# Attention's head norm in a macaron block: squares and last product on GpSimd, inverse roots spread over partitions by DMA

## The chip, the core and the metric

The kernel runs on one core of a Trainium2 chip. Five engines work side by side, each through its own instructions in the program's order: TensorE (PE; its weight loads are shown as PEld), VectorE (DVE), ScalarE (ACT), GpSimd (POOL) and SyncE (SP), which here only issues DMAs. They wait for each other through semaphores. The metric is the device time of one execution in microseconds (us); less is better.

## The reference, cut to what matters

The input x is 8 batches of 512 tokens of 512 values, in float32. Three parts follow each other, each added to x: half of a mixture-of-experts layer, differential attention, and half of the mixture-of-experts layer again. What the change touches is the norm of each head's output in attention:

```python
q, k = _rope(q), _rope(k)
energy = einsum('bqhad,bkhad->bahqk', qd, kd)             # two maps per head
scores = softmax(where(causal, NEG, energy) / sqrt(D))
diff = softmax(where(causal, NEG, scores[:, 0] - lam * scores[:, 1]))
att = einsum('bhqv,bvhd->bqhd', diff, v)                  # 16 heads of D = 32
att = att * rsqrt(mean(att * att, axis=-1) + EPS) * rms_w # the head norm
return (att * (1 - LAM_INIT)).reshape(b, s, E) @ Wo
```

## The kernel before

**Stages.** The first mixture-of-experts layer runs ahead of attention, the second partly beside its end and partly behind it. x stays in SBUF all the time. Attention works through its 8 batches one after the other; each has two phases (head groups gp = 0 and 1) and each phase 11 blocks, 176 blocks in all. A token tile is 128 tokens, so a batch has four tiles (i = 0 to 3); a block holds some heads' queries of one tile against the keys that these may see.

**The loop over blocks** stands in `attention` at L1068 to L1124, and the order of every engine's work is the order in which it is written there (a manual schedule). In round k different blocks are at different steps: scores of block k + 1 (PE, L761), energies of block k (DVE, L777: score plus causal mask, and the smallest value of a row), first exponentials of block k (ACT, L790), mask (POOL, L828), factors (DVE L799, POOL L804) and weighing (POOL, L814) of block k - 1, difference of block k - 1 (DVE, L848), second exponentials of block k - 2 (ACT, L862), transposes of block k - 3 (PE, L882; copies on DVE L898 and ACT L900), and the product with the values of block k - 4 (PE, L913), copied on DVE into the tile "aT" (L926).

**Slots.** All other work of attention is put into named slots of a round: `at(o, slot, fn)` puts fn into round o of a phase, and `fill(k, slot)` runs what is there. In the order of a round the slots are "short" (early on PE), "act mid", "mid", "long", "long 2" (PE), "dve", "act" and "pool". The slot "pool" comes last in a round, behind the difference, and its instructions are made to wait for that difference (`after=u1["diff"]`). So on POOL they stand between the weighing of one block and the mask of the next.

In these slots are: the layer norm of the next batch ("h", L574 on POOL), the projections with rope (`rope_steps`: product "r_ps" L635 on PE, two products with cosine and sine on DVE L654 and L656, two DMAs on SP that swap neighbouring partitions, "r_sw" from "r_by" L662, and an addition on POOL L665), the value projection (L610), and `finish_steps`, which the change is about. PSUM has eight banks; four hold scores, two the transposes, and the two of `misc` go in turn to every product of the slots and to the products with the values.

**The head norm, `finish_steps` (L672 to L747),** runs once per batch and tile, 32 times. "aT" has the heads' values along partitions: partition 32 q + d, four chunks c along the free side, so 16 heads, and 128 tokens.

- square (slot "act", round o0): ACT squares aT into "f_sq" (L683, 128x512) and two small squares of the softmax sums z2 into "f_u" (L685), which carry EPS.
- sums (slot "short", round o1): PE sums the squares over each head's 32 partitions with "hsum" (L694) and adds the EPS part (L700), into "f_ss"; head (c, q) comes out on partition 32 c + q.
- root (slot "act mid", round o1): ACT makes the inverse root as exp(-0.5 ln) into "f_r" (L707, L708).
- turn (slot "short", round o3): PE spreads each head's row over its 32 partitions again, 16 products with one column of the identity that is read with step zero 32 times, into "f_f" in PSUM (L715).
- norm (slot "dve", round o3): DVE multiplies aT by f_f into "f_an" (L723).
- pe (slots "long" and "long 2", round o4): PE multiplies by Wo into "f_o" (L731), and DVE adds the result to x one round later (L737).

The rounds are given where it is called:

```python
finish_steps(at, (0, 1, 2, 4, 5) if b < B else LAST[0], b - 1, 2, sts[b - 1])
finish_steps(at, (3, 5, 5, 7, 8) if b < B else LAST[1], b - 1, 3, sts[b - 1])
...
finish_steps(at, (4, 5, 5, 7, 9), b, 0, sts[b])
finish_steps(at, (6, 7, 7, 9, 10), b, 1, sts[b])
```

Tiles 0 and 1 are finished in the second phase of their batch, tiles 2 and 3 in the first phase of the next; the last batch's tiles 2 and 3 in the drain behind all blocks.

Of the kernel before, what the change touches and what calls it, by code (L numbers as in the profile page):

```python
# [9 lines left out]
F32 = mybir.dt.float32  # L10
# [6 lines left out]
P = 128  # L17
# [24 lines left out]
def macaron_kernel(  # L42
# [61 lines left out]
    nc.vector.tensor_scalar(root_eps, parity, RMS_EPS**0.5, None, ALU.mult)  # L104
    both = keep.tile([P, Q], F32, name="both")
    nc.vector.tensor_tensor(both, of_head[:, 0], of_head[:, 1], ALU.add)
    ln_eps = keep.tile([P, 1], F32, name="ln_eps")
    nc.gpsimd.memset(ln_eps, LN_EPS)

# [43 lines left out]
        "S6 T72 L70 X T73 P1 L73 X S7 P2",  # L153
    )

    LAST = ((0, 1, 1, 2, 3), (3, 4, 4, 5, 6))

    KEPT = 6
    ctx.enter_context(tc.manual_schedule())
# [383 lines left out]
    def attention(f0, f1, home, first_end, projections_end, drain):  # L543
# [128 lines left out]
        def finish_steps(at, os, b, i, st):  # L672

            name = f"f{b}_{i}"
            t = {}

            def square():
                t["sq"] = home["sq"].tile([P, 4, P], F32, name=f"{name}_sq", tag="sq", bufs=2)

                t["u"] = tiny.tile([P, 2, 4, 4], F32, name=f"{name}_u", tag="u")  # L680
                z2 = st["z2"][:, i * H : (i + 1) * H]
                uh = t["u"].rearrange("p f c (q h) -> p (f c q) h", h=2)
                nc.scalar.activation(t["sq"], st["aT"][i], AF.Square)  # L683
                for h in range(2):
                    nc.scalar.activation(  # L685
                        uh[:, :, h], z2, AF.Square, scale=root_eps[:, h : h + 1]
                    )

            def sums():


                t["ss"] = misc(f"{name}_ss")
                for c in range(4):
                    nc.tensor.matmul(  # L694
                        t["ss"][32 * c : 32 * (c + 1), :P], hsum, t["sq"][:, c, :],
                        start=True, stop=False, tile_position=(0, 32 * c),
                    )
                for f in range(2):
                    for c in range(4):
                        nc.tensor.matmul(  # L700
                            t["ss"][32 * c : 32 * c + 4, f * Q : (f + 1) * Q], t["u"][:, f, c],
                            both, start=False, stop=(f == 1), tile_position=(0, 32 * c),
                        )

            def root():
                r = t["r"] = tiny.tile([P, P], F32, name=f"{name}_r", tag="r")
                nc.scalar.activation(r, t["ss"][:, :P], AF.Ln, bias=idle)  # L707
                nc.scalar.activation(r, r, AF.Exp, scale=-0.5)  # L708

            def turn():  # L710

                t["f"] = misc(f"{name}_f")
                for c in range(4):
                    for q in range(4):
                        nc.tensor.matmul(  # L715
                            t["f"][q * D : (q + 1) * D, c * P : (c + 1) * P],
                            ident[:, 32 * c + q : 32 * c + q + 1].to_broadcast([P, D]), t["r"],
                            start=True, stop=True, tile_position=(0, q * D),
                        )

            def norm():
                t["an"] = home["sq"].tile([P, 4, P], F32, name=f"{name}_an", tag="sq", bufs=2)
                nc.vector.tensor_tensor(  # L723
                    t["an"], st["aT"][i], t["f"].rearrange("p (c q) -> p c q", c=4), ALU.mult
                )

            def pe(h):
                if h == 0:
                    t["o"] = misc(f"{name}_o")
                for c in (2 * h, 2 * h + 1):  # L730
                    nc.tensor.matmul(  # L731
                        t["o"], t["an"][:, c, :], wo_sb[:, c // 2, c % 2, :],
                        start=(c == 0), stop=(c == 3),
                    )

            def residual():
                nc.vector.tensor_add(x_sb[b][:, i, :], x_sb[b][:, i, :], t["o"])  # L737

            o0, o1, o2, o3, o4 = os
            at(o0, "act", square)  # L740
            at(o1, "short", sums)
            at(o1, "act mid", root)
            at(o3, "short", turn)
            at(o3, "dve", norm)
            at(o4, "long", lambda: pe(0))
            at(o4, "long 2", lambda: pe(1))
            at(o4 + 1, "mid", residual)  # L747

# [136 lines left out]
        def turn_copy(u, par):  # L887
            nr, i, np = u["nr"], u["i"], u["pairs"]
            o = u["unit"]["eT"][:, par]
            s = u["tp"][par][:, : (i + 1) * nr * P]  # L890
            if nr > np:
                o = o[:, 0].rearrange("p r f t -> p f r t")
                s = s.rearrange("p (f r t) -> p f r t", f=2, r=np)
            else:
                o = o[:, :, :, u["parts"][0].half]
                s = s.rearrange("p (c r t) -> p c r t", c=i + 1, r=nr)
            if par == 0:
                nc.vector.tensor_copy(o, s)  # L898
            else:
                nc.scalar.copy(o, s)  # L900
# [85 lines left out]
        def plan(ph):  # L986

            b, gp = divmod(ph, 2)
            at = placer(starts[ph])
            if gp == 0:  # L990
                if b < B:
                    for n, o in enumerate((0, 0, 1, 2, 3)):
                        rope_steps(at, o, b, 1, n, sts[b])
                    if b + 1 < B:
                        sts[b + 1] = new_batch()
                        norm_steps(at, b + 1, sts[b + 1])
                if b > 0:
                    finish_steps(at, (0, 1, 2, 4, 5) if b < B else LAST[0], b - 1, 2, sts[b - 1])
                    finish_steps(at, (3, 5, 5, 7, 8) if b < B else LAST[1], b - 1, 3, sts[b - 1])
            else:  # L1000
                if b + 1 < B:
                    for n, o in enumerate((0, 1, 1, 2, 4)):
                        rope_steps(at, o, b + 1, 0, n, sts[b + 1])
                    value_steps(at, 3, b + 1, sts[b + 1])
                finish_steps(at, (4, 5, 5, 7, 9), b, 0, sts[b])
                finish_steps(at, (6, 7, 7, 9, 10), b, 1, sts[b])
                if b == B - 1:
                    for n, os in enumerate(EARLY):
                        early_steps(at, n, *os)
# [58 lines left out]
        for k in range(K + 13):  # L1068
# [38 lines left out]
                turn_copy(u2, 0)  # L1107
            if u2 is not None:
                turn_copy(u2, 1)
            fill(k, "long")  # L1110
            if place == 1:
                scores_next(k)
# [89 lines left out]
    def first_end():  # L1202
        first_y.close()
        opened["out"], opened["blocks"] = pool("out", "right"), pool("blocks", "right")
        home.update(aT=opened["out"], sq=opened["out"], h=(opened["out"], "sq"))
        home.update(dict.fromkeys(("kq1", "v", "e", "t", "eT"), opened["blocks"]))

    def projections_end():
# [134 lines left out]
```

## Time and profile before

| what | us |
|---|---|
| median of 3 runs | 1421.32 (1421.29 to 1422.11) |
| profiled execution, from first to last instruction | 1420.2 |
| first layer, start of the projections | 0 to about 210 |
| attention's blocks | about 210 to 1260 |
| rest of the second layer and output | about 1260 to 1420 |

Of the profiled execution only the span is recorded. The operations of the head norm in it:

| operation | engine | count | mean ns |
|---|---|---|---|
| f_sq (L683) | ACT | 32 | 632 |
| f_u (L685) | ACT | 64 | 302 |
| f_ss (L694, L700) | PE | 256, 512 | 283, 222 |
| f_r (L707, L708) | ACT | 32, 32 | 363, 311 |
| f_f (L715) | PE | 1024 | 278 |
| f_an (L723) | DVE | 32 | 683 |
| f_o (L731) | PE | 256 | 605 |

TensorE's instructions overlap, so their count times their mean is more than PE's busy time: f_f takes 35.0 us of PE in all. How to read the views: an engine's busy share is over the whole span; the windows give the same by stage; the chain of work that ended last says, step by step, which piece of work released the next one; in the timeline each line is start, length, engine, line, operation and tiles, and in brackets the idle time ahead of it with what ended it.

### The profile page before, as it was taken

The numbers are of one execution on the slowest core, as the hardware profiler recorded it, in microseconds if no ns is written. First come the engines' busy times: TensorE is split into PE (matmuls) and PEld (weight loads), VectorE is DVE, ScalarE is ACT, GpSimd is POOL, SyncE is SP. The second block draws the span as 40 slices with busy tenths as digits, with TensorE's granted clock in tenths as the row PEclk, the third lists the DMA queues.
The fourth block names the chain that finished last, engine by engine and source line by source line (L and its number), as shares of the span: only waits on it lengthen the run. The fifth ranks groups of instructions, "written<-read, shape, count | busy, mean of one in ns | idle before, by whom it ended". The sixth has DMA issues, their size and how long they took to land.

```text
span 1420.2 us, 30675 instructions
## 1 busy us (share of the span) xinstructions
PE 1328.5 (94%) x9774; PEld 738.4 (52%) x9774; DVE 1154.9 (81%) x4405; ACT 1047.0 (74%) x3644; POOL 685.4 (48%) x1314
## 2 busy tenths in 40 slices
PE   6999899899999999999999999999999997998998
PEld 4544444455555555555555555555455555555443
DVE  6554769899989988998999899889989989654566
ACT  3411128999899898989898998989899989844110
POOL 5433626554555455454545555554545555443230
PEclk9999988999999999999999999999999997999999
DMA  9300011000000101000000001010000001000006
GB/s 344 91 1 0 0 38 38 9 31 24 16 24 17 39 1 38 9 31 9 32 24 16 28 13 39 2 38 16 24 13 27 28 13 40 1 5 1 1 1 236
DMA packets 27554, 48.19 MB, mean 34 GB/s; under 512 B 4720, under 2 KB 6016, under 8 KB 27392
## 3 DMA queue, kind: packets, MB, share of 16 engines
q1 hardware_dynamic: 25152, 42.03, 8.3%
q10 hardware_dynamic: 2208, 4.19, 0.8%
q8 instruction: 77, 1.26, 0.4%
q14 instruction: 85, 0.70, 0.2%
q0 software_dynamic: 32, 0.01, 0.0%
HBM read 16.86 MB, written 8.39 MB: 18 GB/s over the span
## 4 chain that ended last, share of the span: by engine, by line
PE 60%; ACT 13%; DVE 10%; issue 2%; POOL 0%; ACTq 0%; DVEq 0%
PE r_ps L635 18%; PE sc L761 8%; PE f_o L731 8%; ACT e L790 7%; PE tp L882 6%; PE yps L381 6%; PE av L913 4%; DVE e L777 4%; DVE t L848 3%; ACT t L862 2%; PE vps L610 2%; PE kps L403 2%; PE f_f L715 1%; ACT eT L900 1%; PE tp L325 1%
## 5 line engine op out<-in xcount | busy, mean ns | idle before, releaser
L790 ACT ACTIVATE e<-e,nb 128x192 f32<-128x192 f32 (+7 forms) x1024 | 535.5, 532 | 6.5 <-DVE nb L777 4.3
L777 DVE CUSTOM_DVE_ANT_0 e<-sc,mpos 128x192 f32<-128x192 f32 (+7 forms) x1024 | 400.8, 453 | 23.7 <-PE sc L761 16.5
L814 POOL TENSOR_SCALAR e<-e,z 128x512 f32<-128x512 f32 (+7 forms) x512 | 295.9, 590 | 16.7
L862 ACT ACTIVATE t<-t,nm 128x512 f32<-128x512 f32 (+7 forms) x512 | 270.0, 534 | 42.2 <-DVE nm L848 42.0
L761 PE MATMUL sc<-r,r 32*128 32x64 f32 (+7 forms) x2048 | 245.3, 456 | 10.8 <-DVE nb L777 4.9
L848 DVE CUSTOM_DVE_ANT_0 t<-e,z 128x512 f32<-128x512 f32 (+7 forms) x512 | 240.6, 518 | 5.1 <-POOL e L814 4.2
L635 PE MATMUL r_ps<-hT,wq_sb 128*128 128x512 f32 x512 | 235.6, 601 | 0.1
L381 PE MATMUL yps<-we,y 128*128 128x512 f32 x456 | 216.5, 612 | 1.0 <-ACT y L388 0.7
L882 PEld LDWEIGHTS tp<-ident,t 128*128 128x128 f32 x1280 | 146.5, 144 | 135.6 <-ACT eT L900 43.3
L882 PE MATMUL tp<-ident,t 128*128 128x128 f32 x1280 | 188.6, 283 | 28.1 <-ACT eT L900 26.6
L790 ACT ACTIVATION_READ_ACCUMULATOR e<-e,nb 128x1 f32 x1024 | 202.1, 197 | 0.0
L665 POOL TENSOR_TENSOR r<-r,r_sw 128x512 f32<-128x512 f32 x80 | 103.0, 1296 | 175.8 <-DVE z L799 84.2
L761 PEld LDWEIGHTS sc<-r,r 32*128 32x128 f32 x2048 | 117.4, 188 | 90.7 <-DVE nb L777 44.6
L391 POOL TENSOR_TENSOR y<-y,eb 128x512 f32<-128x512 f32 x57 | 73.1, 1283 | 164.4 <-ACT y L388 134.3
L635 PEld LDWEIGHTS r_ps<-hT,wq_sb 128*128 128x128 f32 x512 | 93.0, 190 | 113.9 <-issue 99.6
L388 ACT COPY y<-yps 128x512 f32<-128x512 f32 x57 | 33.4, 586 | 155.6 <-PE yps L381 155.6
L828 POOL TENSOR_SCALAR_AFFINE_SELECT e<-e 128x128 f32<-128x128 f32 x256 | 79.2, 316 | 99.4 <-ACT e L790 99.4
L898 DVE COPY eT<-tp 128x512 f32<-128x512 f32 (+1 forms) x176 | 112.0, 636 | 16.6 <-PE tp L882 16.6
L381 PEld LDWEIGHTS yps<-we,y 128*128 128x128 f32 x456 | 81.3, 192 | 78.4 <-issue 73.6
L731 PE MATMUL f_o<-wo_sb,f_an 128*128 128x512 f32 x256 | 118.6, 605 | 0.0
L804 POOL TENSOR_TENSOR z<-z,over 128x4 f32<-128x4 f32 (+1 forms) x192 | 38.0, 201 | 142.6 <-DVE z L799 142.5
L862 ACT ACTIVATION_READ_ACCUMULATOR t<-t,nm 128x1 f32 x512 | 100.4, 196 | 0.0
(123 smaller groups left out, 1668.6 us busy)
## 6 DMA issues: line engine op xcount, KB each, us to landing
r_sw<-r_by SPq DMA_DIRECT2D x160, 128.0 KB, 2.0
x<-in_x_dram SPq DMA_DIRECT2D x6, 1024.0 KB, 13.2
out_dram<-x SPq DMA_DIRECT2D x6, 512.0 KB, 3.2
out_dram<-x ACTq DMA_DIRECT2D x6, 512.0 KB, 3.2
x<-in_x_dram SPq DMA_DIRECT2D x8, 256.0 KB, 8.2
we<-in_expert_w_dram SPq DMA_DIRECT2D x2, 1024.0 KB, 7.7
wq_sb<-in_wq_dram SPq DMA_DIRECT2D x1, 2048.0 KB, 13.9
wo_sb<-in_wo_dram SPq DMA_DIRECT2D x8, 128.0 KB, 2.8
```

The costliest lines, as they stand in the source:

```text
L381: nc.tensor.matmul(held["yps"], buf[b][:, i, c * P : (c + 1) * P], held["we"][:, c, :], start=(c == 0), stop=(c == EC - 1),)
L635: nc.tensor.matmul(t["ps"], w[:, c, c0 : c0 + P], st["hT"][:, c, :], start=(c == 0), stop=(c == EC - 1),)
L665: return nc.gpsimd.tensor_add(t["out"], t["out"], t["sw"])
L731: nc.tensor.matmul(t["o"], t["an"][:, c, :], wo_sb[:, c // 2, c % 2, :], start=(c == 0), stop=(c == 3),)
L761: nc.tensor.matmul(u["sc"][j][:, part.cols], q[j * D : (j + 1) * D, q0 : q0 + P], kq["k"][j * D : (j + 1) * D, : part.n], start=True, stop ...
L777: nc.vector.tensor_tensor_reduce(out=u["e"][:, j, part.cols], in0=u["sc"][j][:, part.cols], in1=mpos[:, S - part.n :], scale=1.0, scalar=3 ...
L790: nc.scalar.activation(e, e, AF.Exp, bias=u["nb"][:, c : c + 1], scale=-1.0, accum_out=u["z"][:, 0, c : c + 1],)
L814: nc.gpsimd.tensor_scalar(e, e, u["z"][:, 1, c : c + 1], u["z"][:, 0, c - nr : c - nr + 1], ALU.mult, ALU.mult,)
L848: u["diff"] = nc.vector.tensor_tensor_reduce(out=u["t"][:, par, r * w : r * w + part.n], in0=u["e"][:, 2 * par, s], in1=u["e"][:, 2 * par ...
L862: nc.scalar.activation(t, t, AF.Exp, bias=u["nm"][:, par, r : r + 1], scale=-1.0, accum_out=z2[:, col : col + 1],)
L882: nc.tensor.transpose(u["tp"][par][:, o : o + P], u["t"][:, par, (r * (i + 1) + c) * P : (r * (i + 1) + c + 1) * P], ident,)
L898: nc.vector.tensor_copy(o, s)
```

## The change

Thirty of the 32 head norms change; tiles 2 and 3 of the last batch keep the way of before, under the names `square_late`, `turn_late` and `norm_late`. In the others:

- square goes from ACT (slot "act") to POOL (slot "pool", same round): one 128x512 product of aT with itself, a 128x16 product of z2 with itself, and a 128x32 product of that with the new constant "eps_of".
- sums stays in its round or comes one earlier, but goes from the slot "short" to a new slot "sums", behind the transposes' copies and ahead of "long"; root goes from "act mid" to "act".
- turn and its 16 products on PE go. In their place SP issues four DMAs, one per chunk c: four rows of f_r are each written to 32 partitions of f_sq (64 KB). They follow the root in program order.
- norm goes from DVE (slot "dve") to POOL (slot "pool"), in place in f_sq, in the round after the root. That is two to one rounds earlier than before; pe stays where it was.
- The normalised input "h" gets its own buffers; before it shared those of "sq".

```diff
-    LAST = ((0, 1, 1, 2, 3), (3, 4, 4, 5, 6))
+    LAST = ((0, 1, 2, 3), (3, 4, 5, 6))
...
             def square():
                 t["sq"] = home["sq"].tile([P, 4, P], F32, name=f"{name}_sq", tag="sq", bufs=2)
+                first = nc.gpsimd.tensor_tensor(t["sq"], st["aT"][i], st["aT"][i], ALU.mult)
                 z2 = st["z2"][:, i * H : (i + 1) * H]
+                zz = tiny.tile([P, H], F32, name=f"{name}_zz", tag="zz")
+                nc.gpsimd.tensor_tensor(zz, z2, z2, ALU.mult)
+                nc.gpsimd.tensor_tensor(
+                    factor_tile(), zz.unsqueeze(2).to_broadcast([P, H, 2]),
+                    eps_of.unsqueeze(1).to_broadcast([P, H, 2]), ALU.mult,
+                )
+                return first
...
+            def spread():
+                for c in range(4):
+                    nc.sync.dma_start(
+                        t["sq"][:, c, :],
+                        t["r"][32 * c : 32 * c + 4, :].unsqueeze(1).to_broadcast([4, D, P]),
+                    )
+
+            def norm():
+                t["an"] = t["sq"]
+                return nc.gpsimd.tensor_tensor(t["an"], t["an"], st["aT"][i], ALU.mult)
+
-            def turn():
+            def turn_late():
...
-            o0, o1, o2, o3, o4 = os
-            at(o0, "act", square)
-            at(o1, "short", sums)
-            at(o1, "act mid", root)
-            at(o3, "short", turn)
-            at(o3, "dve", norm)
-            at(o4, "long", lambda: pe(0))
...
+            o0, o1, o2, o3 = os
+            if b == B - 1 and i > 1:
+                at(o0, "act", square_late)
...
+            else:
+                at(o0, "pool", square)
+                at(o1, "sums", sums)
+                at(o1, "act", root)
+                at(o1, "act", spread)
+                at(o2, "pool", norm)
+            at(o3, "long", lambda: pe(0))
...
-                    finish_steps(at, (0, 1, 2, 4, 5) if b < B else LAST[0], b - 1, 2, sts[b - 1])
-                    finish_steps(at, (3, 5, 5, 7, 8) if b < B else LAST[1], b - 1, 3, sts[b - 1])
+                    finish_steps(at, (0, 1, 2, 5) if b < B else LAST[0], b - 1, 2, sts[b - 1])
+                    finish_steps(at, (3, 4, 5, 8) if b < B else LAST[1], b - 1, 3, sts[b - 1])
...
-                finish_steps(at, (4, 5, 5, 7, 9), b, 0, sts[b])
-                finish_steps(at, (6, 7, 7, 9, 10), b, 1, sts[b])
+                finish_steps(at, (4, 5, 6, 9), b, 0, sts[b])
+                finish_steps(at, (6, 7, 8, 10), b, 1, sts[b])
...
+            fill(k, "sums")
             fill(k, "long")
...
-        home.update(aT=opened["out"], sq=opened["out"], h=(opened["out"], "sq"))
+        home.update(aT=opened["out"], sq=opened["out"], h=(opened["out"], "h"))
```

## The prediction

> **What bounds the kernel now.** I read four views in this order: the busy shares, the windows by stage, the chain of work that ended last, and the timeline of one engine. The first line of the page:
>
> ```profile
> PE 1328.5 (94%) x9774; PEld 738.4 (52%) x9774; DVE 1154.9 (81%) x4405; ACT 1047.0 (74%) x3644; POOL 685.4 (48%) x1314
> ```
>
> These are means over stages. The change lies in attention, where one batch takes some 130 us (from one matmul of a kind to its twin: 458.87 to 589.00 in the chain). The windows of that batch, each with its length and the busy time of PE, PEld, DVE, ACT, POOL:
>
> ```profile
> 458.00:490.00 32.00, 32.00 (x249) 17.13 (x243) 29.64 (x141) 29.07 (x124) 15.73 (x36) 1.00 0.09 35
> 490.00:529.00 39.00, 35.24 (x348) 20.73 (x344) 36.68 (x143) 35.99 (x117) 21.76 (x44) 1.00 0.02 8
> 529.00:563.00 34.00, 34.00 (x229) 19.64 (x232) 27.61 (x118) 30.90 (x123) 19.32 (x43) 0.95 0.09 32
> 563.00:582.00 19.00, 17.55 (x216) 10.19 (x216) 18.36 (x62) 18.30 (x58) 9.04 (x18) 0.82 0.05 16
> ```
>
> PE has no idle time in the first and third window, so it is the bound there. In the second DVE and ACT fill 94% and 92%, in the fourth 97% and 96%; PE waits there. All four head norms of a batch have their products "f_f" in the second and fourth kind of window, so taking PE work away there gives less than its length. The chain in the fourth window, with start and length:
>
> ```profile
> 564.04 0.31 ACT f_r L708
> ...
> 568.80 0.53 ACT f_sq L683
> 569.33 0.41 ACT f_u L685 x2
> ...
> 580.09 1.41 PE f_f L715 x32
> ```
>
> POOL is idle half the time, but what it does comes late in a loop: exponentials on ACT, mask and weighing on POOL, difference on DVE, second exponentials on ACT. Its order there:
>
> ```profile
> 569.09 1.31 POOL L665 TENSOR_TENSOR r<-r,r_sw 128x512 f32<-128x512 f32 x1 [2.15 <-DVE z L799]
> 570.35 0.29 POOL L828 TENSOR_SCALAR_AFFINE_SELECT e<-e 128x128 f32<-128x128 f32 x1
> 570.61 0.20 POOL L804 TENSOR_TENSOR z<-z,over 128x4 f32<-128x4 f32 x1
> 570.92 1.30 POOL L814 TENSOR_SCALAR e<-e,z 128x384 f32<-128x384 f32 x2
> ```
>
> The rope addition waits for the difference of the block before, and mask and weighing stand behind it. They end at 572.22, and DVE begins the next difference at 572.4: slack 0.2 us. What is put into that place of POOL's order is late at once.
>
> **What goes.** Of 32 head norms 30 change. PE: 35.0 us busy in "f_f" over 32 is 1.09 us each, 33 us. DVE: "f_an" 0.683 us each, 20 us. ACT: "f_sq" 0.632 and two "f_u" of 0.302, 1.24 us each, 37 us. On the chain of one batch stand: f_f 1.01 (449.81), f_f and the wait for f_an (493.34 to 495.09, 1.75), f_sq and f_u 0.94, f_f 1.41. Sum 5.1 us, over 7 batches 36: the most the change could give.
>
> **What comes.** POOL: two 128x512 products of two tiles, priced by the rope addition at 1.296; a 128x16 product 0.214 (the additions to "sum"); a 128x32 product, not shown, between 0.20 (128x8) and 0.41 (128x16, "lsum"), taken as 0.3. Sum 3.1 us each, 93 us; POOL would be busy 778 us, 55%. Rope additions take 1267 to 1319 ns in all 80 cases whatever runs beside them, so I add nothing for contention. SP: four DMAs each, 120 in all, of 0.552 us, on a queue that mostly waits (854.9 us for "r_by"); a rope swap behind them is issued up to 2.2 us later, but it becomes ready some 4 us after a root. Setting up "eps_of" costs nothing that can be seen.
>
> **The places, without waiting for a DMA.** I follow one batch. Fourth window, head norms of tiles 0 and 1: the slot shown above gets tile 0's last product (1.30) and tile 1's squares (1.8) behind the rope addition. Weighing ends 3.1 us later; the difference may start on its first half, so DVE is 2.3 us late. ACT gains 0.94 (f_sq, f_u), DVE 0.69 two blocks on (f_an), and PE's f_f (1.41) falls where DVE is late anyway. Also PE waits there for tile 1's squares some 1 us in "sums". By the next PE-bound stretch (f_o at 582.57) 0.9 us are lost. Second window, tiles 2 and 3: the squares fit (slack 2.9 and 2.8 us between weighing and difference). Tile 2's last product follows two rope additions, slack 0.2, but PE's scores end later than DVE would be ready. At 493.34 f_f waited for a PSUM bank that "r_by" holds; the sums of tile 3 now take that bank and wait for it too, so only f_an and part of f_f are won. I get 0.8 at 505 and 1.3 at 528. Net 0.4 us gained per batch, 3 over 7; the last batch has slack of 1 to 6 us in all these slots and gains some 2. So without a wait: 5 us faster.
>
> **The wait for the spread.** The last product is first in POOL's order after one more block, and now waits for four DMAs that start when the root is done. Behind it stand mask and weighing, for them DVE's difference, ACT's second exponentials and PE's transposes: a wait is paid in full. For each tile I compare the end of the root with the moment POOL would be free. Tile 0: f_ss goes behind eight score matmuls, so the root ends at 565.2 in place of 564.35; POOL ends its rope addition at 570.4: room 5.2. Tile 1: before, the root ended at 574.05 in the chain, now 1 us later for PE's wait, 575.0; POOL is free when the difference ends, 578.4 (timeline) plus the 2.3 from above, 580.7: room 5.75, and then 0.35 of slack before DVE. Tile 3: the bank is free at 493.3, sums 0.65, root 0.68, so 494.65; difference's end 500.4, 0.9 earlier, and a rope addition, 500.8: room 6.15, slack 0.6. Tile 2: the root ended at 474.5, now 0.9 later, 475.4; two rope additions end at 484.3: room 8.9, slack 0.4. So with a landing time T from the root, a batch loses what T is over 5.2, 6.1, 6.75 and 9.3, each counted by itself.
>
> T isn't in this trace. Its rows:
>
> ```profile
> r_sw<-r_by SPq DMA_DIRECT2D x160, 128.0 KB, 2.0
> ...
> eb<-in_expert_b_dram SPq DMA_DIRECT2D x2, 256.0 KB, 8.7
> ...
> lqt<-in_lq_dram SPq DMA_DIRECT2D x2, 256.0 KB, 6.6
> ```
>
> Each spread writes 64 KB from four rows, every row read 32 times; four of them are 256 KB. Three issues come ahead of the last, 3 x 0.55 = 1.65 us. Low end: as the swap between partitions, 1.65 + 2.0 = 3.65. High end: as the loads of one row into all partitions, 1.65 + 8.7 = 10.35 by eb's median, 13.65 by its longest (12.0). I take lqt, also one row for 128 partitions: 1.65 + 6.6 = 8.25. It is nearer in kind than the swap, which repeats nothing; that it reads HBM speaks for less. At 8.25 a batch loses 3.05 + 2.15 + 1.5 + 0 = 6.7, seven batches 47 us.
>
> The trace's swaps run beside each other over all engines: 42.03 MB in 8.3% of 16 engines' 1420 us is 22 GB/s an engine. The Trainium skill, "DMA: Bandwidth & Descriptors", section on why a DMA increments its semaphore by 16, says that a DMA uses the largest number of engines up to 16 that divides the outer size of both sides: here 4 (source 4, target 128). "SBUF — State Buffer", section on door 1, gives four neighbouring partitions one port of about 27 GB/s; no run here shows it. By it 64 KB take 2.4 us, four one after the other 9.7, with 1.6 before the first byte T is 11.3, and the time would be 1541.
>
> **Sum.** The profiled span is 1420.2; -5 + 47 gives 1462; the median of the runs shown is 1.1 above that span, so 1463.
>
> **Rivals.**
> 1. *No wait* (T under 5.3): the DMA lands before POOL is free. 1421 - 5 = 1416, between 1408 and 1424: faster. For it: the swap's 2.0 us, and a queue with room. Against: rows read 32 times over. It decides at T = 5.2, tile 0's room.
> 2. *Long wait* (T over 9.3, all four tiles pay): at 10.35 the loss is 5.15 + 4.25 + 3.6 + 1.05 = 14.05, 98 us, 1514; at 11.6, some way towards eb's longest, 133 us, 1550. For it: eb. Against: eb waited behind other loads.
> 3. *All that leaves the chain is won* (5.1 x 7 = 36): 1385. Against: POOL's slack of 0.2 us.
> That the change doesn't do what it says can be ruled out by its order, which has 30 squares, 120 spreads and 30 products on POOL and SP.
>
> **Chances.** Forecast (T from 5.3 to 9.3, 1424 to 1490) 0.35; long wait 0.30; no wait 0.29; all won 0.06. The range 1408 to 1550 leaves out rival 3 and the far end of rival 2. Faster (by over 0.2%, 2.8 us, about what a measurement of this kernel can tell): 0.06 and 0.17 of rival 1, 0.23; within 0.09; slower 0.68.
>
> **What would show it.** In the profile after, POOL's product of f_sq and aT has idle time before it that a DMA ended: about 3 us for tile 0, 2 for tile 1, 1.5 for tile 3, none for tile 2. The DMA list shows f_sq from f_r with 64 KB and some 6 to 7 us to landing. ACT's and DVE's busy time fall by 37 and 20 us, PE's by about 33, POOL's rises by 93. With landings near 2 us the idle time is gone and rival 1 holds; with landings near 9 or more tile 2 waits as well. Wrong in another way I would be if POOL's products took much more than 1.3 us, or if PE waited long for the sums.

## The result and the profile after

The changed kernel takes 1631.3 us (median of 4 runs, 1626.05 to 1636.79) where the kernel before takes 1421.71 (4 runs on the same chip, 1421.29 to 1423.59): 1.147 times as long, interval 1.1445 to 1.1499. The forecast was 1463 with a range to 1550: the sign was right, the size was not, and the time lies outside the range. The profiled execution ran 1636.79 us with a span of 1635.1.

The page of the changed kernel, busy shares and the row of the granted clock, which goes up and down between 6 and 9 all through attention (9 is the highest digit):

```profile
PE 1404.7 (86%) x8814; PEld 776.5 (47%) x8814; DVE 1140.2 (70%) x4376; ACT 1029.9 (63%) x3554; POOL 770.4 (47%) x1434
...
PEclk9999898888978797979797979796989697899899
```

The same row of the kernel before:

```profile
PEclk9999988999999999999999999999999997999999
```

PE has 960 matmuls less and is busy 76 us more. The costliest groups of instructions (busy, mean ns of one, idle time before them and what ended it) name the place:

```profile
L735 POOL TENSOR_TENSOR f_sq<-f_sq,aT 128x512 f32<-128x512 f32 x30 | 37.9, 1263 | 232.8 <-DMA f_sq<-f_r 232.8
```

The added time is 210 us, and POOL alone waits 232.8 for the spread, in every one of its 30 last products. The list of waits (us in total, times, longest) shows who stands behind it:

```profile
POOL f_sq L735 <- DMA f_sq<-f_r: 232.8, 30, 11.1
DVE t L882 <- POOL e L848: 227.3, 82, 11.1
...
ACT t L896 <- DVE nm L882: 177.2, 108, 8.0
```

In the kernel before DVE hardly waited for POOL there, 4.2 us in all:

```profile
L848 DVE CUSTOM_DVE_ANT_0 t<-e,z 128x512 f32<-128x512 f32 (+7 forms) x512 | 240.6, 518 | 5.1 <-POOL e L814 4.2
```

One such wait, tile 0 in the fourth window, in the timelines of ACT and of POOL (start, length, and in brackets the idle time before and what ended it):

```profile
625.78 0.37 ACT L723 ACTIVATE f_r<-f_ss,idle 128x128 f32<-128x128 f32 x1 [0.90 <-PE f_ss L716]
626.18 0.31 ACT L724 ACTIVATE f_r<-f_r 128x128 f32<-128x128 f32 x1
```

```profile
630.36 1.30 POOL L667 TENSOR_TENSOR r<-r,r_sw 128x512 f32<-128x512 f32 x1 [2.15 <-DVE z L833]
639.58 1.26 POOL L735 TENSOR_TENSOR f_sq<-f_sq,aT 128x512 f32<-128x512 f32 x1 [7.92 <-DMA f_sq<-f_r]
640.80 1.04 POOL L685 TENSOR_TENSOR f_sq<-aT 128x512 f32<-128x512 f32 x1
641.79 0.21 POOL L688 TENSOR_TENSOR f_zz<-z 128x16 f32<-128x16 f32 x1
642.09 0.24 POOL L689 TENSOR_TENSOR f_u<-f_zz,eps_of 128x32 f32<-128x32 f32 x1
642.28 0.29 POOL L862 TENSOR_SCALAR_AFFINE_SELECT e<-e 128x128 f32<-128x128 f32 x1
```

The root ends at 626.49, the product starts at 639.58: T is 13.1 us. POOL is free at 631.66, 5.2 after the root, as the forecast had it, and then stands still for 7.9. The squares of tile 1, mask and weighing are queued behind. Of the 13.1 us, 1.3 pass from the root to the first packet of the spread, 11.3 from there to the end of its last packet, and 0.5 until the product starts.

Over all batches, T and the idle time before the product, by tile. The room is the time from the end of the root to the moment at which the product could start without the spread: POOL's work before it is done, and the difference for which its slot waits has ended.

| tile | T, us | room forecast | room measured | POOL idle | idle beyond the room |
|---|---|---|---|---|---|
| 0 | 13.23 | 5.2 | 5.25 | 8.50 | 7.99 |
| 1 | 13.07 | 5.75 | 6.14 | 9.78 | 6.93 |
| 3 | 13.10 | 6.15 | 5.60 | 7.50 | 7.50 |
| 2 | 13.59 | 8.9 | 8.73 | 4.86 | 4.86 |

The idle times add up to 30.6 us a batch, 27.3 of them beyond the room. (Ahead of tile 1's product POOL stands still for some 2.7 us in any case, until the difference has ended; e1_no_spread below, which has no spread, shows it too.) PE's windows in the same batch (length, busy PE, PEld, DVE, ACT, POOL, granted clock, DMA share, GB/s) show what the wait does to PE:

```profile
634.00:641.00 7.00, 0.00 (x0) 0.00 (x0) 0.00 (x0) 0.51 (x3) 1.42 (x2) 0.53 0.14 16
641.00:658.00 17.00, 15.92 (x81) 8.98 (x82) 8.58 (x29) 9.67 (x28) 6.57 (x14) 0.50 0.14 17
```

Seven microseconds without a matmul, and then 17 at half the clock. Whether that second part costs time as well is a question for the experiments.

### The profile page after: what moved, and what is told of

It is laid out like the page before. It is cut to its first block, busy times and chain, and to the rows that moved or that the text cites. A ratio compares the mean times of both kernels' runs of the same rounds, so it can differ in the third digit from the quotient of the medians.

```text
span 1635.1 us, 29094 instructions
## 1 busy us (share of the span) xinstructions
PE 1404.7 (86%) x8814; PEld 776.5 (47%) x8814; DVE 1140.2 (70%) x4376; ACT 1029.9 (63%) x3554; POOL 770.4 (47%) x1434
## 3 DMA queue, kind: packets, MB, share of 16 engines
q1 hardware_dynamic: 40992, 49.90, 11.4%
q10 hardware_dynamic: 2208, 4.19, 0.7%
## 4 chain that ended last, share of the span: by engine, by line
PE 43%; DMA 17%; DVE 11%; POOL 8%; ACT 6%; issue 2%; POOLq 0%; DVEq 0%; ACTq 0%
DMA f_sq<-f_r 17%; PE r_ps L637 12%; PE sc L795 7%; PE tp L916 5%; PE yps L383 5%; PE f_o L758 5%; DVE e L811 5%; ACT e L824 4%; POOL e L848 4%; DVE t L882 3%; PE av L947 2%; POOL f_sq L735 2%; PE vps L612 2%; PE kps L405 2%; ACT t L896 1%
## 5 line engine op out<-in xcount | busy, mean ns | idle before, releaser
L795 PE MATMUL sc<-r,r 32*128 32x192 f32 (+7 forms) x2048 | 294.6, 515 | 28.4 <-DVE nb L811 23.3
L848 POOL TENSOR_SCALAR e<-e,z 128x512 f32<-128x512 f32 (+7 forms) x512 | 308.1, 615 | 16.7
L916 PEld LDWEIGHTS tp<-ident,t 128*128 128x128 f32 x1280 | 161.3, 154 | 118.5 <-issue 44.1
L916 PE MATMUL tp<-ident,t 128*128 128x128 f32 x1280 | 200.1, 301 | 13.0 <-ACT eT L934 11.8
L795 PEld LDWEIGHTS sc<-r,r 32*128 32x128 f32 x2048 | 145.4, 208 | 115.5 <-DVE nb L811 70.9
L824 ACT ACTIVATION_READ_ACCUMULATOR e<-e,nb 128x1 f32 x1024 | 196.1, 191 | 0.0
L735 POOL TENSOR_TENSOR f_sq<-f_sq,aT 128x512 f32<-128x512 f32 x30 | 37.9, 1263 | 232.8 <-DMA f_sq<-f_r 232.8
L758 PE MATMUL f_o<-wo_sb,f_sq 128*128 128x512 f32 x240 | 137.3, 723 | 0.0
L932 DVE COPY eT<-tp 128x512 f32<-128x512 f32 (+1 forms) x176 | 111.9, 636 | 16.2 <-PE tp L916 16.2
L710 PE MATMUL f_ss<-f_sq,hsum 128*32 128x128 f32 x256 | 17.1, 348 | 102.7 <-POOL f_sq L685 55.8
L934 ACT COPY eT<-tp 128x512 f32<-128x512 f32 (+1 forms) x176 | 94.1, 535 | 15.2 <-PE tp L916 14.8
```

Of the source, the lines that this page charges most:

```text
L758: nc.tensor.matmul(t["o"], t["an"][:, c, :], wo_sb[:, c // 2, c % 2, :], start=(c == 0), stop=(c == 3),)
L795: nc.tensor.matmul(u["sc"][j][:, part.cols], q[j * D : (j + 1) * D, q0 : q0 + P], kq["k"][j * D : (j + 1) * D, : part.n], start=True, stop ...
L824: nc.scalar.activation(e, e, AF.Exp, bias=u["nb"][:, c : c + 1], scale=-1.0, accum_out=u["z"][:, 0, c : c + 1],)
L848: nc.gpsimd.tensor_scalar(e, e, u["z"][:, 1, c : c + 1], u["z"][:, 0, c - nr : c - nr + 1], ALU.mult, ALU.mult,)
L916: nc.tensor.transpose(u["tp"][par][:, o : o + P], u["t"][:, par, (r * (i + 1) + c) * P : (r * (i + 1) + c + 1) * P], ident,)
```

## Experiments

Theory A: the loss is POOL's wait for the spread, and T is long because the four rows that a spread reads lie next to each other. Rivals: B, the added work and its place in POOL's order cost much by themselves; C, the transfer is slow whatever rows it reads; D, the halved clock behind the wait is a large part. Later A' (others wait behind the spread on SP's queue) and E (a gain is given back through the clock) came to it. The kernel before ran beside each group: 1421.7 to 1422.3.

**Without the spread.** The line `at(o1, "act", spread)` is taken out.

> Leaves out the four spread DMAs of each head norm: POOL's last product takes the squares themselves in place of the spread roots (so the head norm's factor is left out of the output); every other instruction and its place stays. Theory A (the loss is POOL's wait for the spread, and what follows from that wait): no idle time that a DMA ended before f_sq and aT, 1408 to 1430 us, clock back to about 0.96. Rival B (POOL's own added work and PE's waits for squares, 63.1 + 55.8 us before f_ss in the changed kernel, cost much by themselves): 1460 us or more, and those waits stay. Rival C (the transfer is slow in itself, whatever rows it reads): as A.

1446.79 us (1.0171, interval 1.0143 to 1.0199), clock 0.939: between the two expectations. The spread costs 1631.3 - 1446.8 = 184.5 us, so A holds for most of the loss. But 25 us stay without any wait for the spread, where the forecast had 5 us of gain. PE's matmuls no longer wait for squares (0.1 us at most ahead of the sums of tile 1, after 8.0 on the mean of seven batches), so B in the form "PE waits for squares" falls; that the places cost something stays.

**Roots four partitions apart.**

```
-            pattern=[[-D * mult, 32]], ...                  # hsum: one row a head
+            pattern=[[0, 2], [-D * mult, 4], [0, 4]], ...   # head q on rows 4q
-                        t["r"][32 * c : 32 * c + 4, :].unsqueeze(1)...
+                        t["r"][32 * c : 32 * c + 16 : 4, :].unsqueeze(1)...
```

(Beside it "u" is 16 columns wide with zeros between, in one kept tile; "idle" is zero; "nb" has two buffers, for room.)

> Same work, same output: the sums are written 16 rows wide, and the root of head q of chunk c lies on partition 32c+4q in place of 32c+q, so each spread reads four rows four partitions apart. Theory A with one port (four neighbouring rows are read through one port; 4 packets of 512 B in flight at 74 ns each are 27.7 GB/s): packets fall to the 27 ns of the other transfers, T from 13.1 to some 4.5 us (three issues at 0.55, 1.25 to the first packet, 0.9 for 32 packets of each engine, 0.5 for the semaphore), the wait of 232.8 us falls below 40, time 1416 to 1440. Rival C (512-B packets from SBUF to SBUF on four engines are slow whatever the rows): packets stay near 74 ns, T near 13, time 1615 to 1640. Rival B: T falls as in A, but the time stays over 1460.

1460.12 us (1.0267, 1.0252 to 1.0283): outside A's 1416 to 1440, at the edge of B's 1460. The wait is nearly gone:

```profile
POOL f_sq L735 <- DMA f_sq<-f_r: 3.5, 6, 1.4
```

The page's line on SP's queue (packets, MB, share of 16 engines' span), first the changed kernel, then this one:

```profile
q1 hardware_dynamic: 40992, 49.90, 11.4%
```

```profile
q1 hardware_dynamic: 40992, 49.90, 10.0%
```

The same packets and bytes: 11.4% of 16 x 1635.1 us is 2982 us, 10.0% of 16 x 1457.1 is 2331, 651 less over 15,360 packets of the spread, 42 ns each. The records of single packets say the same: median 74 ns with neighbouring rows, 27 with rows four apart, with three or four in flight in the first and five or six in the second. In the changed kernel 22 packets of 512 B start in half a microsecond, 22.5 GB/s; here 82, 84 GB/s. One spread of a tile, first issue to last packet: 626.5 to 639.1 before the edit, 579.1 to 583.6 with it. Which four rows are read decides, so C falls. The Trainium skill, "SBUF — State Buffer", section "Door 1: The DMA port swizzle", gives four neighbouring partitions one port and rows four apart a port each; the two runs agree. Its 27 GB/s is a fifth above the 22.5 measured, and the measurement decides.

The time is 38 us above the kernel before with the spread fast, of which 25 stand in e1_no_spread as well: what B says of the places holds for these. The other 13 us come with only 3.5 us of waiting; measured as in the block table below they lie mainly in blocks 17, 20 and 11 (0.5, 0.9 and 0.4 us a batch), and were not taken apart further.

**The product later.** Its round is moved by two for tiles 0, 2 and 3, by one for tile 1: `(0, 1, 4, 5)`, `(3, 4, 7, 8)`, `(4, 5, 8, 9)`, `(6, 7, 9, 10)`.

> The last product is put two blocks later for tiles 0, 2 and 3 and one block later for tile 1; the spread is unchanged. A block lasts some 5.9 us (130 us over 22). Theory A: T stays 13.1; the rooms grow from 4.7, 5.6, 8.7 to 16 or more, wait 0; tile 1's from 3.3 to 9.2, wait 3.9; seven batches lose 27 us: 1435 to 1460. Rival B: over 1480. Rival C: as A.

1426.3 us (1.0024, 1.0012 to 1.0036), with the packets still at 74 ns and the wait at 21.7 us in 5 places, all of them tile 1's product. A slow spread that is hardly waited for costs almost nothing. It is better than A expected.

**Squares alone.** Squares on POOL and the sums in their new slot; zero-step products and DVE's product as before, at rounds 3, 6, 7 and 9.

> One part alone: squares and the two small products on POOL with the sums where the change has them; the spread and POOL's last product are undone (zero-step products on PE and the product on DVE, one block after the change's last product, as before). Theory A: the squares alone cost little: 1410 to 1430. Rival B (PE's waits for squares in the sums are a loss of their own): 1450 or more.

1437.37 us (1.011, 1.0095 to 1.0125), 15 us more than before and between the two expectations. Two of these products fall a round earlier than before and tile 3's sums too, so not all of it is the squares'.

**Spread and product alone, product later.** e3_later with

```
-                at(o0, "pool", square);  at(o1, "sums", sums)
-                at(o1, "act", root);     at(o1, "act", spread)
+                at(o0, "act", square_late);  at(o1, "short", sums)
+                at(o1, "act mid", root);     at(o1, "act mid", spread)
```

> The spread and POOL's last product alone, the product in the later places of e3_later; squares and the two factors go back to ACT, sums and root to the places of the kernel before. If the squares' cost (15 us in e4_squares) adds up with the rest: 1426 - 15 = 1411, between 1402 and 1418, so faster than before. Rival: with the product out of the way the squares were already free, and the time stays at e3_later's 1422 to 1430.

1617.54 us (1.1377, 1.136 to 1.1394). Neither: what counts has moved to another wait. The group of the rope additions:

```profile
L667 POOL TENSOR_TENSOR r<-r,r_sw 128x512 f32<-128x512 f32 x80 | 102.9, 1295 | 363.0 <-DMA r_sw<-r_by 153.3
```

In SP's order the spread now stands ahead of the rope swap of its round. In one round SP issues the four spreads from 514.99 to 521.57, the last two in 2.4 and 2.9 us instead of 0.54, and only then the swaps, the first two until 527.44; the spread's packets go on to 528, and most of the swaps' come then. Two engines wait for them, DVE for a buffer of "r_by" that the swap has not read yet, and POOL, in another round, for the swapped values; the timelines of DVE and of POOL:

```profile
529.19 0.69 DVE L658 SCALAR_TENSOR_TENSOR r_by<-r_ps,cst 128x512 f32<-128x512 f32 x1 [9.63 <-DMA r_sw<-r_by]
```

```profile
636.98 1.29 POOL L667 TENSOR_TENSOR r<-r,r_sw 128x512 f32<-128x512 f32 x1 [11.77 <-DMA r_sw<-r_by]
```

The forecast had said of the changed kernel that a swap behind the spread "becomes ready some 4 us after a root"; there this held (4.6 us of such waits), and by an earlier root it no longer holds.

**Matmuls in the idle time** (theory D). In the changed kernel 12 and 9 matmuls go ahead of the sums of tiles 1 and 3, into the sums' own bank:

```
+                for _ in range({1: 12, 3: 9}.get(i, 0) if b < B - 1 else 0):
+                    nc.tensor.matmul(t["ss"], ident, cosk, start=True, stop=True)
```

> The changed kernel, and ahead of the sums of tile 1 and tile 3, where PE stood still 8.0 and 6.4 us for squares, 12 and 9 matmuls of 128x512 (0.6 us each) whose result is overwritten; they fit into the idle time. Theory D (PE's granted clock halves after some us without work, and the slower matmuls behind it are a second loss): clock from 0.876 to 0.92 or more, time lower by 4 to 8 us a batch, 1575 to 1605. Rival (the chain behind the wait goes over DVE and ACT, so the halved clock costs little): 1622 to 1640.

1739.05 us (1.2194): a badly made experiment. The 9 of tile 3 first waited for the bank and then stood in the way (block 4 from 4.2 to 12.5 us), and the 12 overran. It is made again with 8 for tile 1 alone:

> e6_filler mended: in it 12 and 9 matmuls overran the idle time (the 9 of tile 3 waited for the bank first). Now 8 for tile 1 alone. Theory D: clock up by 0.02 or more and 2 to 6 us less a batch, 1590 to 1615. Rival (the next spread, not PE, ends that stretch, so the halved clock of the changed kernel costs little): 1622 to 1640.

1634.92 us (1.1495, 1.1478 to 1.1512), clock 0.893. The clock rises by 0.017 and the time does not fall. From tile 0's product to tile 1's, the stretch behind the wait, 16.0 us pass in the changed kernel, all of them at half the clock, and 16.2 here, 9.3 of them at half the clock (means of three batches). So D falls for this stretch: it ends with the next spread, not with PE. The stretches behind the other waits were not tested by themselves.

**The product early, squares on ACT, no spread.** e1_no_spread with squares, sums and root in the slots of e5_spread_alone; the product stays early.

> e1_no_spread with squares and factors back on ACT, sums and root in the places of before: no spread (the head norm's factor is left out of the output), POOL's last product in its early place. If squares and early product add up: 1447 - 15 = 1432, between 1426 and 1439. Rival (they collide in the one slot of block 17, which takes tile 0's last product and tile 1's squares, so that either alone is cheap): 1410 to 1424.

1436.47 us (1.0107, 1.0092 to 1.0122), as expected if the parts add up. So of the 25 us of e1_no_spread 14.7 come with the product in its early place and 10.3 with the squares.

**The zero-step products as dead work.** e3_later, and `at({0: 7, 1: 9, 2: 4, 3: 7}[i], "short", turn_late)`.

> e3_later with the zero-step products of the kernel before issued again in their old rounds, their result used by nobody. Theory D as to what the change takes from PE (the products that went had kept the clock up; before 0.969, e3_later 0.950): clock 0.962 or more, and the time not above 1424 in spite of 33 us of added matmuls. Rival (they are only work): 1432 to 1455.

1438.73 us (1.0109, 1.0079 to 1.0139), clock 0.948 to 0.956 over the four executions (e3_later 0.946 to 0.951). They are only work; it was not they that had kept the clock up to 0.969.

**The queue of SP** (theory A'). e5_spread_alone with the roots four partitions apart, and e5_spread_alone with the spread issued behind the swap: `at(o1, "act", spread)` in place of `"act mid"`.

> e5_spread_alone with the roots of e2_four_ports, four partitions apart. In e5_spread_alone POOL waited 153.3 us for rope swaps that stand behind the spread on SP's queue. Theory A' (the slow spread, T of 13, fills that queue, and whoever stands behind it waits): with packets of 27 ns the queue is free after some 3 us, the wait for r_sw goes below 20 us, and what was expected of e5_spread_alone holds: 1411, between 1402 and 1418, faster than before. Rival (ACT's earlier root and squares, not the queue, made e5_spread_alone slow): over 1440.

> e5_spread_alone with the four spread DMAs issued at the end of the round, behind the rope swap of the same round, and still from neighbouring rows (packets of 74 ns). Theory A': the swap of the same round goes ahead, but a swap of the next round, some 6 us later, still meets a spread that takes 13: the wait for r_sw falls to about half or less, time between 1415 and 1530. Rival (ACT's earlier root and squares): stays at 1600 or more.

1445.2 us (1.016, 1.0146 to 1.0173) and 1420.41 (0.9992, 0.9975 to 1.0009). POOL's waits for the swap fall as A' says in both:

```profile
  DMA r_sw<-r_by: 15.9, 5
```

```profile
  DMA r_sw<-r_by: 7.7, 4
```

But the time of the first is the rival's, not A's. The second settles it: ACT has the root and the squares as early there, and the loss is gone, so it is the order on the queue.

The order on the queue is worth more than the speed of what is in it. With short spreads (e9_alone_ports) SP stands at the first one until the root is done, then issues four, and swaps that were ready go out at 485.0; in e12_behind_ports below, which differs from it by this order alone, they go out at 470.9, 5.8 us earlier when both are counted from the end of block 0's difference (483.5 and 475.2). With slow spreads behind the swap there is no difference from before, though tile 1's product waits for its spread in seven batches:

```profile
POOL f_sq L735 <- DMA f_sq<-f_r: 32.9, 7, 5.0
```

The twelve executions of e10_alone_behind go with their mean clock, from 1427.77 us at 0.943 to 1414.43 at 0.969. The trace is of the first of these; why they differ was not found.

**Both.**

> e10_alone_behind (1420.4) with the roots four partitions apart, so that the spread is short and stands behind the rope swap of its round as well. If what is left of SP's queue in e10_alone_behind (512-B packets at 64 ns) still costs: 1405 to 1416, faster than before. Rival (in e10_alone_behind the spread is out of the way already; e9_alone_ports was slow by its order on SP's queue alone): 1416 to 1424, no difference from before.

1421.54 us in the median (0.9974, 0.9953 to 0.9996): the rival. Nothing waits for the spread any more and POOL waits 4.6 us for swaps, 33 us of PE's products are gone, and at most half a per cent is won. The twelve times lie in two groups, five from 1411.65 to 1413.17 and seven from 1421.47 to 1425.56, with the same mean clock (0.956 to 0.958 and 0.952 to 0.959); the trace is of the second group, and what parts them is open.

**Where that gain goes** (theory E). The time from the end of one block's difference on DVE to that of the next, mean of batches 1 to 6, for the blocks in which the kernels differ most:

| block | before | changed | e1 | e7 | e10 | e12 | e13 | e15 |
|---|---|---|---|---|---|---|---|---|
| 2 | 7.48 | 12.94 | 7.89 | 7.96 | 7.39 | 7.42 | 7.43 | 7.43 |
| 3 | 6.96 | 5.39 | 5.88 | 5.58 | 6.08 | 6.07 | 6.07 | 6.07 |
| 4 | 4.25 | 4.16 | 4.24 | 4.25 | 5.47 | 5.49 | 5.48 | 5.49 |
| 5 | 5.36 | 12.77 | 5.94 | 5.43 | 5.17 | 4.80 | 4.48 | 4.48 |
| 17 | 4.63 | 15.15 | 6.97 | 5.49 | 4.16 | 4.19 | 4.18 | 4.19 |
| 18 | 4.61 | 4.55 | 4.55 | 4.55 | 5.23 | 4.91 | 6.41 | 4.80 |
| 19 | 5.14 | 11.71 | 4.69 | 4.71 | 4.67 | 4.65 | 4.62 | 4.66 |
| 20 | 5.67 | 5.28 | 7.73 | 8.49 | 7.91 | 7.53 | 5.86 | 6.26 |
| all 22 | 129.69 | 158.55 | 133.40 | 132.21 | 130.50 | 130.05 | 129.24 | 128.76 |

Of the kernels with the product on POOL e1, e7, e10 and e12 are slow in block 20, and not all for one reason. In e10_alone_behind tile 1's product waits there for its slow spread, 4.3 to 5.0 us, and the clock in the block is 1.00 in all six batches. In e12_behind_ports no product waits for a spread, and the mean of 7.53 is made of two kinds of batch: in three of the six a halved stretch of the clock reaches 3.7 to 4.4 us into the block, which takes 8.9 to 9.2 us, and in the other three none does, and it takes 5.9 to 6.3. PE's timeline in one of the three long ones, and its windows:

```profile
577.70 0.55 PE L916 MATMUL tp<-ident,t 128*128 128x128 f32 x3 [1.17 <-ACT eT L934]
578.18 3.65 PE L795 MATMUL sc<-r,r 32*128 32x512 f32 x8
581.76 5.73 PE L758 MATMUL f_o<-wo_sb,f_sq 128*128 128x512 f32 x8
```

```profile
574.00:579.00 5.00, 3.83 (x41) 2.21 (x34) 4.54 (x16) 5.00 (x16) 2.42 (x6) 1.00 0.20 52
579.00:586.00 7.00, 7.00 (x12) 2.85 (x10) 5.16 (x18) 7.00 (x21) 4.81 (x9) 0.51 0.00 1
```

The eight "f_o" of tile 0 take 5.73 us at half the clock; the same eight in the kernel before, where the halved stretch had ended:

```profile
582.50 3.70 PE L731 MATMUL f_o<-wo_sb,f_an 128*128 128x512 f32 x8
```

So two matmuls were put into PE's idle time in rounds 19 and 20, into the bank of the transposes (e13_warm; e14_before_warm is the control), and then into a free bank (e15_warm_misc, control e16_before_warm_misc):

```
+                if par and blocks.index(u) % 22 in (16, 17):
+                    idle_bank = misc(f"warm{u['id']}")        # e13, e14: u["tp"][par]
+                    for _ in range(2):
+                        nc.tensor.matmul(idle_bank, ident, cosk, start=True, stop=True)
```

> e12_behind_ports, and in rounds 19 and 20 of a batch two matmuls of 128x512 ahead of the second half of the transposes, into the same bank, which the transposes then overwrite: PE stands still there for 1.3 and 1.2 us. In e12_behind_ports a batch is 1.9 us ahead of before up to round 19 and loses 1.9 in round 20, where the granted clock is 0.50 from 579.5 to 585.6 and f_o of tile 0 takes 5.7 us in place of 3.7. Theory E (what the change gains is given back there, by the halved clock that follows PE's idle time): clock 1.00 in that stretch, round 20 from 7.5 to 5.7 us, 7 x 1.8 = 13 us less, 1403 to 1413. Rival (another engine ends round 20): 1416 to 1428.

> The kernel before with the same added matmuls in the same rounds. There the clock is 0.50 from 574 to 581, where PE has less to do, and round 20 takes 5.7 us already. Theory E: the time changes by less than 6 us, 1414 to 1426. Rival (matmuls there gain as much in any kernel): 1402 to 1412.

> e13_warm mended: there the clock stayed 1.00 and round 20 fell from 7.53 to 5.86 us as expected, but the added matmuls waited for the bank of the transposes and put round 18 from 4.91 to 6.41. Now they go into a bank that is free (one of misc). Theory E: round 20 stays near 5.9, round 18 goes back to 5.0 to 5.4; 1.2 us or more a batch less than e12_behind_ports, 1406 to 1416. Rival (the transposes' second half is late whatever stands there): 1418 to 1428.

> The same added matmuls in the kernel before, as a control. Theory E (the halved clock costs before nothing in round 20): 1416 to 1430. Rival: before gains as much as e15_warm_misc does, 1403 to 1412.

e13_warm: 1424.98 us (1.0029, 1.0016 to 1.0042), in the rival's range; e14_before_warm: 1438.66 (1.0108, 1.0095 to 1.0122), above both of its ranges. The clock does what E says, and so does "f_o":

```profile
584.00:590.00 6.00, 6.00 (x24) 2.85 (x23) 5.95 (x19) 5.62 (x18) 4.49 (x9) 1.00 0.01 1
```

```profile
586.03 3.70 PE L758 MATMUL f_o<-wo_sb,f_sq 128*128 128x512 f32 x8
```

Block 20 falls from 7.53 to 5.86 and is the same in all six batches, but the added matmuls waited for their bank and block 18 gives 1.5 back. With the free bank: e15_warm_misc 1417.73 us (0.9974, 0.9965 to 0.9983), e16_before_warm_misc 1425.21 (1.0026, 1.0016 to 1.0035). Block 20 takes 6.25 to 6.27 us in all six batches of e15_warm_misc, with no halved stretch in it.

So E is right in its mechanism for block 20 of e12_behind_ports, and its size was put too high: 1406 to 1416 was expected. That the whole gains is not shown. Against the kernel before that ran beside it, e15_warm_misc has the same ratio as e12_behind_ports, 0.9974; the medians are 3.8 us apart, but the means, 1418.5 and 1417.8, only 0.6, because of the two groups in e12_behind_ports. (The three long batches have 3 us each too much, 9 together, which is the distance of the two groups; whether that is what parts them, no trace shows.)

The control is 3.5 us slower than the kernel before beside it, within E's range, but this does not show that the added matmuls win nothing there. In the traces, batches 1 to 6 are 0.6 us a batch shorter with them in the kernel before (129.69 to 129.12) and 1.3 in the new arrangement (130.05 to 128.76). The last batch, which gets them too, is longer by 4.9 in the kernel before (146.3 to 151.3) and by 3.3 in the new arrangement (144.7 to 147.9); in the control this outweighs the gain. The last batch without them was not run. Both e12_behind_ports and e15_warm_misc are faster than the kernel before, by 0.3% each.

## Why the prediction was wrong

**Sign and place: right.** The wait of POOL's last product for the spread sets the time, it is paid nearly in full (206 us of POOL's 232.8 us of idle time lie beyond the room, and 184.5 are lost), and DVE, ACT and PE stand behind it in the order that the forecast gave.

**The step that failed first: T.** The forecast took "lqt", 6.6 us to landing, because it also gives one row to 128 partitions, and got 8.25. Measured are 13.1 to 13.6. The row was chosen for its shape; what limits is where the source lies. "lqt" reads HBM; the spread reads four neighbouring SBUF rows 32 times each, and e2_four_ports shows that the neighbourhood is what costs: from 12.6 to 4.5 us between first issue and last packet. With the measured T in the forecast's own formula a batch loses 8.0 + 7.0 + 6.35 + 4.3 = 25.65, seven batches 180 in place of 47: 133 us of the error. The issues were mis-sized too: three at 0.55 us were counted, and the third and fourth took 2.3 and 2.8 while the slow packets were under way; the packets set the landing, though. The sentences that went by the page on SBUF had T at 11.3 and 1541, nearer than the row that was used.

**The step that failed second: 5 us of gain without a wait.** e1_no_spread has 25 us of loss: 30 of the error. The prices of the operations were not at fault: squares 1.04 us (1.296 forecast), last product 1.26 (1.296), the small ones 0.21 and 0.24 (0.214 and 0.3). At fault was what they do in their places. For tiles 0 and 1 the forecast lost 0.9 us a batch; blocks 17 to 20 lose 3.9. Its first figure was right: DVE 2.3 us late, as block 17 is. But it took 1.4 of this as made good by the work that ACT and DVE lose, and blocks 18 and 19 make good 0.5; and block 20, in which it saw nothing, loses 2.1 more. For tiles 2 and 3 it won 1.3, and blocks 2 to 5 win 0.1. In block 20 of e1_no_spread a halved stretch of the clock covers 2.0 to 4.4 us in every batch; that it is the cause there as in e12_behind_ports is likely, but was not tested. e7_product_early, e10_alone_behind and e1_no_spread divide the 25 us: about 16 for the early place of the product (1436.5 against 1420.4, the second with the spread and its waits), 10 for the squares.

Together 1463 + 133 + 30 = 1626; 5 us of 1631 are left. The rooms were right within 0.6 us for all four tiles.

**The most that could be won.** 5.1 us a batch, 36 in all, was read off the chain. With no wait for the spread in the way (e12_behind_ports, the execution in the trace) the batch is 0.4 us slower than before over its 22 blocks, without the halved clock in block 20 (e15_warm_misc) 0.9 faster. Blocks 3, 5, 17 and 19 win 2.7 together in e15_warm_misc; block 4 gives 1.2 back with the product in it, block 20 0.6. Why removed work on the chain brings so little is shown only for block 20 of e12_behind_ports; the rest stays open.

**Busy times.** POOL rose by 85 us (93 forecast). DVE fell by 15 (20), ACT by 17 (37): e7_product_early has the squares and "f_u" on ACT again and is busy only 19.3 us more than e1_no_spread, 0.64 a norm, about the price of "f_sq" alone. The two "f_u" were counted at 0.302 each, but 0.41 together on the forecast's own chain: durations that partly lie over their neighbours' are not all busy time. PE rose by 76 instead of falling by 33, with the clock at 0.876 after 0.969; e11_filler_few shows that in one stretch a batch the slower matmuls cost nothing.

**Rivals.** "Long wait" was the right one and its range too short: it stopped at T = 11.6, "some way towards eb's longest", while the high end of the rows, 13.65, was in the text. At 13.65 the formula gives 27.3 a batch and 1607. The range should have gone there.

## What to carry to other kernels

A broadcast by DMA out of few SBUF rows is priced by the bytes that it reads, repeats included, through the place where the rows lie; lay the rows apart before anything else, and take rows of the trace as a price only if they read from the same memory. Put what consumes a DMA late in an in-order engine's queue and the DMA itself behind those that are needed first: here putting the consumer one or two rounds later won 205 us (e3_later), making the transfer three times as fast 171 (e2_four_ports). And when work leaves PE, look at the granted clock behind the new gap before counting the gain.

## What was not expected of the hardware

The granted clock has two values here, 1.00 and 0.50, and a halved stretch can follow short gaps: in e12_behind_ports PE stood still for 1.4 us at 571.9 and 1.2 us at 576.5, and from 579.0 to 585.9 the clock was 0.50 though PE had no gap from 577.7 on. Matmuls in such gaps kept it at 1.00 in that block (e13_warm). But it need not follow: batch 1 has the same gap of 1.2 us and no halved stretch behind it. The Trainium skill, "TensorE: Matmul & The Clock Gate", Part 1, also has two states, the slow one after an idle window of about 3.4 us; these gaps were shorter than that.

A DMA issue on SP takes 0.54 to 0.61 us, and 2.0 to 3.0 when slow transfers are under way on its queue (median 2.04 us over the 120 issues in e3_later, 0.54 in e2_four_ports). POOL squares a tile in 1.04 us, a product of two different tiles of that size takes it 1.26.
